# Attention's weight products: seven float32 quarter products replaced by three passes of 11-bit parts

## The chip, the cores and the metric

The kernel runs on one core of one Trainium2 chip. The metric is the time of one launch in microseconds (us), the median of several runs. All engines of the core work from their own instruction queues: TensorE (PE, with its weight loads shown apart as PEld), VectorE (DVE), ScalarE (ACT), GpSimd (POOL) and SyncE (SP, here a queue for DMAs).

## The reference

One transformer layer on 8192 tokens of 256 features, float32 in and out. `x` is `[4, 2048, 256]`; chunks are of 32 tokens.

```python
Q, K, V = x @ W_q.T, x @ W_k.T, x @ W_v.T
S = einsum('bncd,bnkd->bnck', Qc, Kc) * mask        # within chunks of 32, mask = decay ** distance
O = einsum('bnck,bnkd->bncd', S, Vc)
out = (sigmoid(x @ W_g.T) * O) @ W_o.T + x
x = layernorm(x + out)
h = silu(x @ wg.T) * (x @ wu.T)                     # 768 hidden, weights are integers / 127
x = layernorm(x + h @ wd.T)
```

## The kernel before

The tokens are taken in 16 blocks of 512. A block goes through attention two to three blocks ahead of its feed-forward part, so that one pass of the main loop (`b`) holds the feed-forward of block `b`, the scores, values and output product of block `n = b + 2`, and the weight products of block `m = b + 3`.

There are four attention weight products for each block, and they are what is changed. `y = M x` replaces Q and K (`M` is made once from both weights, `make_m`), `g` is the gate, `v` the values and `o` the output product. Feature-major products (`g`, `y`, helper `feature_major`, L455) leave features on partitions; token-major ones (`v`, `o`, helper `token_major`, L473) leave tokens on partitions. For block 0, and for the output product of blocks 0 and 15, they are plain float32 products of whole tiles (`attn_gate` L570, `attn_y` L589, `attn_v` L610, `attn_residual` through `project_back` L677, tile `pa`).

For the other blocks they go through `seven`: both factors are cut into 2 by 2 quarters, and seven float32 quarter products take the place of eight. `weight_sums` makes the sums of a weight's quarters once (POOL, five instructions of 128x128); `token_sums` makes four sums of 128x256 for each block of tokens (POOL), once for `x` and once for the gated values `goT`. `seven` opens four PSUM banks (`p1`, `p6`, `p5`, `p7`), runs four products, lets ACT copy two of the banks (L505) and DVE add them up (L507, L508) and POOL write one quarter of the result (L517); the closure `others` that it gives back runs the last three products onto the banks later and finishes the other quarters (L523, L526, L529, and L551 for the gate's sigmoids). Between the two halves of a set other PE work is put by hand.

The feed-forward part (`ffn_up` L790, `ffn_down` L677 and L856) already works with split operands: hidden states and activations are stored as a rounded high part (`F32R`, in the trace fp32r) and a rest in float16, and each product is run for both. In the trace a float32 product leaves two MATMUL rows and an fp32r or float16 product leaves one; MATMUL rows of fp32r operands are labelled f32 too, and are known by their tiles (`..._hi`).

The order within a queue is a scheduler's, but calls through `in_turn` keep the program's order on their engine, and `in_steady_turn` does so from block 1 on. The order of PE around the change is this, per pass of the loop:

```python
ffn_up(b, hT, uT, range(0, 1)); ffn_up(b, hT, uT, range(1, 2)); sT = attn_scores(n, yT)
ffn_up(b, hT, uT, range(2, 3)); v_next, v_rest = split_v(m, x_sums)
multiply = ffn_up(b, hT, uT, range(3, 4), held=True); v_rest(); multiply()
goT = attn_values(n, sT, v, sg); go_sums = token_sums(goT, f"go_{n}")
y_next, y_rest = split_y(m, x_sums); ffn_up(b, hT, uT, range(4, KH)); y_rest()
sg_next, g_rest = split_gate(m, x_sums); hs[n], out_rest = split_out(n, go_sums)
g_rest(); mv_h = out_rest()
x_sums = token_sums(xTs[m + 1], f"x_{m + 1}", in_turn); ffn_down(...)
```

Ahead of the loop, blocks 0 to 2 go through the same steps, with the weights' sums made first; PE is kept warm by six matmuls of zeros (`WARM`, L185) until the first data has landed.

Of the kernel before, what the change touches and what calls it, by code (L numbers as in the profile page):

```python
# [47 lines left out]
F32 = mybir.dt.float32  # L48
# [6 lines left out]
P = 128  # L55
# [3 lines left out]
TB = 512  # L59
# [7 lines left out]
HALF = 0.5  # L67
WARM = 512, 512, 128
# [3 lines left out]
def kernel(  # L72
# [353 lines left out]
    def weight_sums(w, name):  # L426

        a11, a21 = w[:, 0, :P], w[:, 0, P:]
        a12, a22 = w[:, 1, :P], w[:, 1, P:]
        t = const.tile([P, 5, P], F32, tag=f"{name}_sums", name=f"{name}_sums")  # L430
        s1, s2, s3, s4, minus = (t[:, i, :] for i in range(5))
        nc.gpsimd.tensor_tensor(s1, a21, a22, ALU.add)
        nc.gpsimd.tensor_tensor(s3, a11, a21, ALU.subtract)
        nc.gpsimd.tensor_tensor(s2, s1, a11, ALU.subtract)
        nc.gpsimd.tensor_tensor(s4, a12, s2, ALU.subtract)
        nc.gpsimd.tensor_scalar(minus, a22, -1.0, None, ALU.mult)
        return a11, a12, s4, minus, s1, s2, s3

    def token_sums(t, name, order=free):

        out = sums.tile([P, 4, HB], F32, tag=f"{name[0]}_sums", name=f"{name}_sums")
        t1, t3, t2, t4 = (out[:, i, :] for i in range(4))
        b11, b12, b21, b22 = (t[:, k, n * HB : (n + 1) * HB] for k in range(2) for n in range(2))
        order(nc.gpsimd.tensor_tensor(t1, b12, b11, ALU.subtract))
        nc.gpsimd.tensor_tensor(t3, b22, b12, ALU.subtract)
        nc.gpsimd.tensor_tensor(t2, b22, t1, ALU.subtract)
        nc.gpsimd.tensor_tensor(t4, t2, b21, ALU.subtract)
        return b11, b21, b22, t4, t1, t2, t3

    def feature_major(a, b):  # L450


        def product(i, pb, first, order=free):
            order(
                nc.tensor.matmul(  # L455
                    pb,
                    lhsT=a[i - 1],
                    rhs=b[i - 1],
                    start=first,
                    stop=True,  # L460
                    skip_group_check=True,
                )
            )

        return product

    def token_major(a, b):


        def product(i, pb, first, order=free):  # L470
            for g in range(HB // P):
                order(
                    nc.tensor.matmul(  # L473
                        pb[:, g * P : (g + 1) * P],
                        lhsT=b[i - 1][:, g * P : (g + 1) * P],
                        rhs=a[i - 1],
                        start=first and g == 0,
                        stop=True,
                        skip_group_check=True,
                    )  # L480
                )

        return product

    def seven(name, product, quarter, func=AF.Copy, plus=None):

        def shaped(t, like):
            return t.rearrange("p (g d) -> p g d", d=P) if len(like.shape) == 3 else t

        def part(what):
            return sums.tile([P, HB], F32, tag=what, bufs=2, name=f"{what}_{name}")

        banks = {i: bank(f"p{i}_{name}")[:, :HB] for i in (1, 6, 5, 7)}
        p = {}  # L500
        for i, pb in banks.items():
            product(i, pb, True)
            if i in (1, 5):
                p[i] = part(f"p{i}")
                nc.scalar.copy(p[i], pb)  # L505
        u, p57 = part("p6"), part("p57")
        in_steady_turn(nc.vector.tensor_tensor(u, banks[6], p[1], ALU.add))  # L507
        in_steady_turn(nc.vector.tensor_tensor(p57, banks[7], p[5], ALU.add))  # L508
        c11, c12, c21, c22 = (quarter(i, j) for i in range(2) for j in range(2))
        to_c12 = to_c21 = u  # L510
        if plus is not None:
            x11, x12, x21, x22 = (plus(i, j) for i in range(2) for j in range(2))
            to_c12, to_c21 = part("to_c12"), part("to_c21")
            for t, xq in ((to_c12, x12), (to_c21, x21)):
                nc.gpsimd.tensor_tensor(shaped(t, xq), shaped(u, xq), xq, ALU.add)
            nc.gpsimd.tensor_tensor(shaped(p57, x22), shaped(p57, x22), x22, ALU.add)
        nc.gpsimd.tensor_tensor(c22, shaped(p57, c22), shaped(u, c22), ALU.add)  # L517

        def others():
            for i, onto in ((2, 1), (3, 5), (4, 7)):  # L520
                product(i, banks[onto], False, in_turn)
            if plus is None:
                nc.scalar.activation(c11, shaped(banks[1], c11), func)  # L523
            else:
                in_steady_turn(
                    nc.vector.tensor_tensor(c11, shaped(banks[1], c11), x11, ALU.add)  # L526
                )
            for c, pb, t in ((c12, banks[5], to_c12), (c21, banks[7], to_c21)):
                in_steady_turn(nc.vector.tensor_tensor(c, shaped(pb, c), shaped(t, c), ALU.add))  # L529

        return others

    def by_features(t):
        return lambda i, j: t[:, i, j * HB : (j + 1) * HB]

    def by_tokens(t):
        per = NG // 2
        return lambda i, j: t[:, j * per : (j + 1) * per, i * P : (i + 1) * P]


    w_sums = {}

    def split_gate(b, x_sums):
        sg = work.tile([P, KD, TB], F32, tag="sg", name=f"sg_{b}")
        product = feature_major(w_sums["g"], x_sums)
        others = seven(f"g_{b}", product, by_features(sg), AF.Sigmoid)

        def rest():
            others()
            for raw in (sg[:, 0, HB:], sg[:, 1, :]):  # L550
                nc.scalar.activation(raw, raw, AF.Sigmoid)  # L551

        return sg, rest

    def split_y(b, x_sums):
        yT = work.tile([P, KD, TB], F32, tag="yT", name=f"yT_{b}")
        return yT, seven(f"y_{b}", feature_major(w_sums["m"], x_sums), by_features(yT))

    def split_v(b, x_sums):
        v = work.tile([P, NG, D], F32, tag="v", name=f"v_{b}")  # L560
        return v, seven(f"v_{b}", token_major(w_sums["v"], x_sums), by_tokens(v))

    def attn_gate(b):
# [4 lines left out]
        for ec in range(KD):  # L568
            for dc, pg in enumerate(banks):
                product = nc.tensor.matmul(  # L570
                    pg,
                    lhsT=wg[:, ec, dc * P : (dc + 1) * P],
                    rhs=xt[:, ec, :],
                    start=(ec == 0),
                    stop=(ec == KD - 1),
                )
                in_turn(product)
# [4 lines left out]
    def attn_y(b, beside=None):  # L582
# [3 lines left out]
        for fc in range(KD):  # L586
            py = bank(f"py_{b}_{fc}")
            for ec in range(KD):
                nc.tensor.matmul(  # L589
                    py,  # L590
                    lhsT=m_sb[:, ec, fc * P : (fc + 1) * P],
# [9 lines left out]
    def attn_v(b):  # L601
# [3 lines left out]
        for h in range(NG // per):  # L605
            pv = bank(f"pv_{b}_{h}")
            for j in range(per):
                g = h * per + j
                for ec in range(KD):
# [3 lines left out]
                        rhs=wv[:, ec, :],  # L613
# [31 lines left out]
    def attn_values(b, sT, v, sg):  # L645
        goT = work.tile([P, KD, TB], F32, tag="goT", name=f"goT_{b}")
# [45 lines left out]
    def attn_residual(b, goT):  # L692
# [7 lines left out]
        project_back(b, (chunked(goT),), (chunked(wo),), residual, "pa")  # L700
# [7 lines left out]
    def split_out(b, goT_sums):  # L708
# [3 lines left out]
        product = token_major(w_sums["o"], goT_sums)  # L712
        others = seven(f"o_{b}", product, by_tokens(r), plus=by_tokens(xn))

        def rest():
            others()
            return moments(r, f"a{b}")
# [183 lines left out]
    table = const.tile([P, 1], F32, tag="table", name="table")  # L901
    hs, hTs = {}, {}
    sg, v = attn_gate(0), attn_v(0)
    for w, name in ((wg, "g"), (wv, "v")):
        w_sums[name] = weight_sums(w, name)
    x_sums = token_sums(xTs[1], "x_1")
    make_m()
    w_sums["m"] = weight_sums(m_sb, "m")
    in_turn(nc.scalar.mul(wo, wo, HALF))
    w_sums["o"] = weight_sums(wo, "o")  # L910
    sg_1, g_rest = split_gate(1, x_sums)
    fg = integers(ffn_gT, ffn_int[0], "fg")
    look_up([0])
    yT = attn_y(0, lambda half: look_up([1 + half]))
    g_rest()
    look_up([3])
    v_1, rest = split_v(1, x_sums)
# [4 lines left out]
    yT, rest = split_y(1, x_sums)  # L922
# [3 lines left out]
    hs[0] = attn_out(0, goT)  # L926
    sT_1 = attn_scores(1, yT)
    xTs[3] = load_xT(3)
    x_sums = token_sums(xTs[2], "x_2")
    v, rest = split_v(2, x_sums)  # L930
    goT = attn_values(1, sT_1, v_1, sg_1)
    go_sums = token_sums(goT, "go_1")
    rest()
    yT, rest = split_y(2, x_sums)
# [3 lines left out]
    hs[1], out_rest = split_out(1, go_sums)  # L938
    sg, g_rest = split_gate(2, x_sums)
# [12 lines left out]
    for b in range(NB - 2):  # L952
# [12 lines left out]
        if b == 0:  # L965
            g_rest()
            x_sums = token_sums(xTs[m], f"x_{m}")
# [12 lines left out]
        if more:  # L980
            v_next, v_rest = split_v(m, x_sums)
# [10 lines left out]
        if b == 1:  # L992
            count = count_wide()
            n_wide_early = const.tile([1, 1], I32, tag="n_wide_early", name="n_wide_early")
            nc.vector.tensor_copy(n_wide_early, count)
        if more:
            go_sums = token_sums(goT, f"go_{n}")
            y_next, y_rest = split_y(m, x_sums)
# [318 lines left out]
```

## Time and profile before

| what | value |
|---|---|
| time of a launch, median of 3 runs | 524.65 us (523.93 to 524.71) |
| span of the profiled execution, first to last instruction | 522.4 us |
| what lies around the span (median less span) | 2.25 us |
| PE busy | 515.8 us, 99% |
| DVE, POOL, ACT busy | 389.8, 343.5, 320.4 us |
| mean granted TensorE clock | 0.998 |
| one pass of the loop, in the middle of the run | 31.6 us |
| busy in the pass from 233.60 to 265.20 | PE 31.60, DVE 23.49, ACT 19.85, POOL 21.80 us |

The page gives the profiled execution no other time than its span. "Chain" is the chain of work that ended last, followed back from the last instruction. Rows of a group give how many instructions there were and the mean time of one in ns; PE's rows overlap, because its matmuls are pipelined, so PE's cost is read from start to start or from the chain.

### The profile page before, as it was taken

To read this page: it belongs to the slowest core of one execution; us is meant where nothing else is said; L and a number is where in the kernel's file an instruction comes from. 1 tells how busy PE (TensorE), PEld (TensorE's weight loads), DVE (VectorE), ACT (ScalarE), POOL (GpSimd) and SP (SyncE) were. 2 spreads that over 40 slices of the span, in tenths; PEclk is the share of its full clock that TensorE was granted. 3 is DMA by queue.
4 is the path that set the end of the run, shared out by engine and by line. 5 is a ranking of instruction groups with operands and counts; after the bars stand their busy time and mean duration, and the time that the engine had idled before them with its cause. 6 is when DMAs were issued, how large, how long until landed. Compare 5 with 4: busy or idle time off the path is not lost.

```text
span 522.4 us, 10573 instructions
## 1 busy us (share of the span) xinstructions
PE 515.8 (99%) x3648; PEld 421.8 (81%) x3648; DVE 389.8 (75%) x965; ACT 320.4 (61%) x644; POOL 343.5 (66%) x475
## 2 busy tenths in 40 slices
PE   9999999999999999999999999999999999999995
PEld 5798887887978788887888878889787888878685
DVE  3978797686776867868677776877868677787876
ACT  2755565465656756666675665656566566667746
POOL 6535785776847668485675856678486685836554
PEclk9999999999999999999999999999999999999999
DMA  7721121213213131131311313141121311102102
GB/s 246 234 83 43 51 62 29 63 42 76 89 32 90 52 112 41 39 95 45 106 43 45 119 25 97 44 117 43 35 89 51 110 43 40 44 21 62 62 23 81
DMA packets 43320, 36.90 MB, mean 71 GB/s; under 512 B 4864, under 2 KB 39168, under 8 KB 43264
## 3 DMA queue, kind: packets, MB, share of 16 engines
q1 hardware_dynamic: 42144, 35.28, 22.6%
q10 hardware_dynamic: 1120, 0.92, 0.5%
q8 instruction: 30, 0.49, 0.4%
q14 instruction: 26, 0.21, 0.1%
HBM read 20.45 MB, written 8.39 MB: 55 GB/s over the span
## 4 chain that ended last, share of the span: by engine, by line
PE 98%; DVE 1%; ACT 0%; issue 0%
PE fg L790 17%; PE fu L790 16%; PE fdn L677 14%; PE p_v L473 9%; PE p_y L455 9%; PE p_g L455 9%; PE p_o L473 8%; PE po L651 5%; PE ps L630 3%; PE fdn L856 2%; PE pa L677 1%; PE pi L185 1%; PE pv L610 1%; PE pg L570 1%; PE py L589 1%; PE fdn L1125 1%
## 5 line engine op out<-in xcount | busy, mean ns | idle before, releaser
L815 POOL TENSOR_TENSOR u_lo<-u,u_hi 128x512 f16<-128x512 f32 (+1 forms) x98 | 122.9, 1256 | 111.2 <-ACT u_hi L814 109.7
L814 ACT CAST u_hi<-u 128x512 fp32r<-128x512 f32 (+1 forms) x98 | 59.7, 609 | 67.0 <-DVE u L812 66.6
L800 DVE SCALAR_TENSOR_TENSOR s<-fg,s 128x512 f32<-128x512 f32 (+1 forms) x98 | 66.2, 677 | 33.5 <-ACT s L798 33.4
L798 ACT ACTIVATE s<-fg 128x512 f32<-128x512 f32 (+1 forms) x98 | 55.9, 582 | 40.7 <-PE fg L790 40.7
L812 DVE TENSOR_TENSOR u<-fu,s 128x512 f32<-128x512 f32 (+1 forms) x98 | 66.5, 679 | 10.4 <-POOL u_lo L815 1.1
L790 PE MATMUL fg<-hT_hi,fg_hi 128*128 128x512 f32 (+1 forms) x196 | 73.8, 458 | 0.0
L790 PE MATMUL fu<-hT_hi,fu_hi 128*128 128x512 f32 (+1 forms) x196 | 60.5, 390 | 0.0
L790 PE MATMUL fg<-hT_lo,fg_lo 128*128 128x512 f16 (+1 forms) x196 | 57.9, 377 | 0.0
L790 PE MATMUL fu<-hT_lo,fu_lo 128*128 128x512 f16 (+1 forms) x196 | 57.4, 375 | 0.0
L677 PE MATMUL fdn<-fd_hi,u_hi 128*128 128x256 f32 x312 | 45.7, 288 | 0.0
L790 PEld LDWEIGHTS fu<-hT_hi,fu_hi 128*128 128x128 f32 x196 | 36.5, 188 | 8.4
L410 ACT ACTIVATE h<-h,shift_h,scale_h 128x256 f32<-128x256 f32 x52 | 27.0, 590 | 24.1 <-POOL shift_h L373 24.1
L790 PEld LDWEIGHTS fg<-hT_hi,fg_hi 128*128 128x128 f32 x196 | 34.6, 189 | 8.9
L677 PEld LDWEIGHTS fdn<-fd_hi,u_hi 128*128 128x128 f32 x312 | 38.9, 189 | 0.3
L677 PE MATMUL fdn<-fd_lo,u_lo 128*128 128x256 f16 x312 | 38.6, 273 | 0.0
L790 PEld LDWEIGHTS <-fu_lo 128*128 128x128 f16 x196 | 19.2, 98 | 22.2
L773 POOL TENSOR_TENSOR hT_lo<-hT,hT_hi 128x512 f16<-128x512 f32 x28 | 35.3, 1280 | 1.2 <-ACT hT_hi L772 1.2
L838 DVE SCALAR_TENSOR_TENSOR r<-fdn,h 128x512 f32<-128x512 f32 x30 | 20.7, 689 | 20.4 <-PE fdn L677 18.0
L790 PEld LDWEIGHTS <-fg_lo 128*128 128x128 f16 x196 | 15.3, 98 | 20.7 <-issue 12.9
L473 PE MATMUL p_v<-v_sums,x_sums 128*128 128x128 f32 x240 | 31.8, 275 | 0.0
L677 PEld LDWEIGHTS <-u_lo 128*128 128x128 f16 x312 | 28.4, 98 | 3.9
L651 PE MATMUL po<-sT,v 128*128 128x128 f32 x256 | 31.2, 275 | 0.0
(210 smaller groups left out, 1182.7 us busy)
## 6 DMA issues: line engine op xcount, KB each, us to landing
x<-in_x_dram SPq DMA_DIRECT2D x16, 512.0 KB, 3.4
xT<-in_xT_dram SPq DMA_DIRECT2D x15, 512.0 KB, 4.2
hT<-sq SPq DMA_DIRECT2D x224, 32.0 KB, 1.9
out_dram<-r SPq DMA_DIRECT2D x13, 512.0 KB, 4.5
out_dram<-r SPq DMA_DIRECT2D x7, 128.0 KB, 1.7
fg_int<-in_ffn_gT_dram SPq DMA_DIRECT2D x3, 256.0 KB, 8.5
fu_int<-in_ffn_uT_dram SPq DMA_DIRECT2D x3, 256.0 KB, 7.2
fd_int<-in_ffn_dT_dram SPq DMA_DIRECT2D x3, 256.0 KB, 5.9
```

The source lines that it names most:

```text
L410: nc.scalar.activation(r[:, g, :], r[:, g, :], AF.Identity, bias=shift[:, g : g + 1], scale=scale[:, g : g + 1],)
L455: nc.tensor.matmul(pb, lhsT=a[i - 1], rhs=b[i - 1], start=first, stop=True, skip_group_check=True,)
L473: nc.tensor.matmul(pb[:, g * P : (g + 1) * P], lhsT=b[i - 1][:, g * P : (g + 1) * P], rhs=a[i - 1], start=first and g == 0, stop=True, ski ...
L651: nc.tensor.matmul(po[:, cols], lhsT=v[:, g, dc * P : (dc + 1) * P], rhs=sT[:, cols], start=True, stop=True,)
L677: nc.tensor.matmul(pb[:, j * D : (j + 1) * D], lhsT=part[:, g * P : (g + 1) * P], rhs=w, start=(i == 0), stop=(i == len(terms) - 1),)
L773: nc.gpsimd.tensor_tensor(in_order[1], whole, in_order[0].bitcast(F32), ALU.subtract)
L790: nc.tensor.matmul(pb, lhsT=w[kind][:, dc, hc * P : (hc + 1) * P], rhs=hT[kind][:, dc, cols], start=(kind == kinds[0] and dc == 0), stop=( ...
L798: order(nc.scalar.activation(s, pg, AF.Sigmoid, scale=SCALE / H_UP))
L800: gated = nc.vector.scalar_tensor_tensor(s, pg, U_UP / H_UP**2, s, ALU.mult, ALU.mult)
L812: in_steady_turn(nc.vector.tensor_tensor(u, pu, s, ALU.mult))
L814: nc.scalar.copy(hi, u)
L815: nc.gpsimd.tensor_tensor(lo, u, hi.bitcast(F32), ALU.subtract)
```

## The change

Each operand is split into a high part, rounded to fp32r, and a scaled low part. The product is `hi*hi + lo*lo` and a third product of differences that supplies both mixed terms (Karatsuba): three passes, each over the whole operand, all in fp32r. After the first two passes the PSUM bank is scaled in place by ACT (`WHOLE`), and the third pass is added onto it. The sets are used where `seven` was, and also for the output product of block 15, where `attn_residual` was.

```diff
+SHIFT = 2.0**12
+TOP = 1.0 - 0.5 / SHIFT
+WHOLE = 1.0 + 1.0 / SHIFT
...
+    def weight_parts(w, name, tags):
+        hi, lo = (const.tile([P, KD, D], F32R, ...) ...)
+        nc.scalar.mul(hi, w, TOP)
+        nc.gpsimd.tensor_tensor(lo, w, hi.bitcast(F32), ALU.subtract)
+        nc.gpsimd.tensor_scalar(lo, lo.bitcast(F32), SHIFT, None, ALU.mult)
+        return [hi, lo]
+
+    def weight_gap(parts, name):
+        nc.gpsimd.tensor_tensor(gap, hi.bitcast(F32), lo.bitcast(F32), ALU.subtract)
+        parts.append(gap)
+
+    def token_parts(t, name, order=free):
+        for k in range(KD):
+            order(nc.scalar.mul(hi[:, k, :], t[:, k, :], TOP))
+            whole = hi[:, k, :].bitcast(F32)
+            order(nc.gpsimd.tensor_tensor(lo[:, k, :], t[:, k, :], whole, ALU.subtract))
+            in_steady_turn(
+                nc.vector.scalar_tensor_tensor(
+                    gap[:, k, :], whole, -WHOLE, t[:, k, :], ALU.mult, ALU.add
+                )
+            )
...
     def feature_major(a, b):
+        def product(i, pb, kind, order=free):
+            for k in range(KD):
+                order(nc.tensor.matmul(pb, lhsT=a[kind][:, k, i * P : (i + 1) * P],
+                                       rhs=b[kind][:, k, :], start=kind + k == 0, ...))
     def token_major(a, b):
+        per = TB // D
+        def product(i, pb, kind, order=free):
+            for k in range(KD):
+                for j in range(per):
+                    g = i * per + j
+                    order(nc.tensor.matmul(pb[:, j * D : (j + 1) * D],
+                                           lhsT=b[kind][:, k, g * P : (g + 1) * P],
+                                           rhs=a[kind][:, k, :], start=kind + k + j == 0, ...))
-    def seven(name, product, quarter, func=AF.Copy, plus=None):
...
+    def three(name, product, finish):
+        banks = [bank(f"p{i}_{name}") for i in range(2)]
+        for i, pb in enumerate(banks):
+            product(i, pb, 0)
+            product(i, pb, 1)
+            in_steady_turn(nc.scalar.mul(pb, pb, WHOLE))
         def others():
+            for i, pb in enumerate(banks):
+                product(i, pb, 2, in_turn)
+                finish(i, pb)
         return others
...
-    for w, name in ((wg, "g"), (wv, "v")):
-        w_sums[name] = weight_sums(w, name)
-    x_sums = token_sums(xTs[1], "x_1")
+    for name in ("wg", "wv"):
+        w_parts[name] = weight_parts(given[name], name, (f"{name}_hi", f"{name}_lo"))
+        weight_gap(w_parts[name], name)
+    x_parts = token_parts(xTs[1], "x_1")
...
-            hs[n] = attn_residual(n, goT)
-            mv_h = moments(hs[n], f"a{n}", order=in_turn)
+            hs[n], out_rest = split_out(n, go_parts)
+            mv_h = out_rest(in_turn)
```

`finish` is a sigmoid by ACT for `g` (two of 128x512), a copy by DVE for `y`, a copy by ACT for `v`, and an addition of `x` by DVE for `o`. The tile `goT` has one buffer where it had two. A branch that runs only for integer weights above 128 gets its float32 weights back from the parts; with these inputs it does not run.

## The prediction

> **What bounds the kernel now.** I read the busy shares first, then the chain by engine, then the chain in order of time for one pass of the loop, then PE's timeline for the pace of fp32r, and last the groups by form for the other engines. Busy shares and chain of the page:
>
> ```profile
> PE 515.8 (99%) x3648; PEld 421.8 (81%) x3648; DVE 389.8 (75%) x965; ACT 320.4 (61%) x644; POOL 343.5 (66%) x475
> PE 98%; DVE 1%; ACT 0%; issue 0%
> ```
>
> PE never waits; a change pays as far as it shortens PE's work, and costs as far as it makes PE wait. The chain in order of time (start, us) shows what PE spends in a pass on the weight products:
>
> ```profile
> 13.79 1.73 PE p_g L455 x8
> ...
> 245.82 1.78 PE p_v L473 x16
> 249.40 1.34 PE p_v L473 x12
> 250.74 1.79 PE po L651 x16
> 252.52 1.73 PE p_y L455 x8
> 257.86 1.29 PE p_y L455 x6
> ...
> 265.30 5.43 PE fdn L677 x48
> ...
> 487.21 0.47 PE fu L790 x2
> 487.68 0.45 PE fg L790 x2
> 488.12 0.43 PE fu L790 x2
> ```
>
> A feature-major set costs 1.73 + 1.29 = 3.02 us, a token-major one 1.78 + 1.34 = 3.12. The last three lines give the pace of 512 columns: two fp32r matmuls in 0.47, two float16 ones in 0.43 to 0.45. For 256 columns PE's timeline has, start to start (1.50 us for twelve fp32r):
>
> ```profile
> 235.47 1.65 PE L677 MATMUL fdn<-fd_hi,u_hi 128*128 128x256 f32 x12
> 236.97 1.48 PE L677 MATMUL fdn<-fd_lo,u_lo 128*128 128x256 f16 x12
> ```
>
> **PE's work.** A set becomes three passes over whole operands. Feature-major: 3 x 2 banks x 2 = 12 matmuls of 512 columns, 12 x 0.235 = 2.82 us, 0.20 less. Token-major: 24 of 256 columns. Their price lies between 0.113 (5.43 / 48, half of it float16) and 0.125 (1.50 / 12); I take 0.12, since `u_hi` is loaded as these weights will be: 2.88 us, 0.24 less. Blocks 1 to 15 have `y`, `g`, `v`: 30 x 0.20 + 15 x 0.24; `o` runs for 14 blocks: 14 x 0.24; block 15's `pa` goes from 3.46 to 2.88. Sum 6.0 + 3.6 + 3.4 + 0.6 = **13.6 us less**; at 0.125 and 0.113 it is 10.0 and 18.6.
>
> **The other engines, per pass.** POOL loses eight token sums, four corner sums and three additions of x, 15 x 0.73 = 11.0, and gains four low parts of 1.28: 21.8 becomes 15.9. DVE loses 17 additions of 0.42 and gains four gaps, two copies of `y` and two additions of `x` at about 0.68: 23.5 becomes 21.8. ACT loses eight copies (0.37), three finishes (0.38) and two sigmoids (0.42, 0.63), 5.1 us, and gains eight scalings, two sigmoids and two copies at 0.585 and four high parts at 0.61, 9.5 us: 19.9 becomes 24.2 of 30.7. No engine becomes the bound by its sum. The 0.585 is this row, which reads PSUM and writes SBUF; no row has ACT writing PSUM:
>
> ```profile
> L617 ACT COPY v<-pv 128x512 f32<-128x512 f32 x2 | 1.2, 585 | 1.3 <-PE pv L610 1.3
> ```
>
> The bounds are 0.55 (the pace of neighbouring ACT rows) and 0.69 (DVE on the same bank). [...]
>
> **The new waits, start.** Before, block 1's gate set starts at 13.79, on sums that POOL had made by 14.1 as they were needed. Now, by the order in the program, POOL makes the low parts of two weights, scales both, makes both gaps, and only then `x_1_lo`. Each is 128x512: a subtraction 1.28; a scaling has no row: 128x128 takes 0.525 and 128x4 0.22, so 1.47 by that slope, bounds 1.28 (a subtraction) and 2.1 (four times 0.525). ACT's first table load stands behind the landing of `wg` (about 5.4): load 1.28, `wg_hi` 0.62, done at 7.3; `wv_hi` stands behind a second load and the decay (9.2): 9.8. POOL: `wg_lo` at 8.6, `wv_lo` 11.1, two scalings 14.0, two gaps 16.6, `x_1_lo` 17.9 and 19.1. PE finishes the two `hi` matmuls at 14.26, waits 3.6 us, runs one, waits 1.0: **4.6 us** (bounds 3.9 and 5.9). Behind it on PE all is queued in order. Later, `x_2_hi` stands behind ACT's casts of the integer weights and `x_2_lo` (two of 1.28) behind it: 0.5 us. The scalings of the other early sets end before PE asks.
>
> The idle PE brings in its clock. At the end of the run the last matmul ended at 516.8, and the windows read 1.00 until 520, 0.97 to 520.5 and then:
>
> ```profile
> 520.50:521.00 0.50, 0.00 (x0) 0.00 (x0) 0.00 (x0) 0.00 (x0) 0.00 (x0) 0.50 0.81 268
> ```
>
> So 3.7 us of idleness halved it. Here the unbroken wait is 3.6: I take no drop, but it is at the edge; the six warm-up matmuls took 4.18 us where full pace gives 2 x 0.86 + 0.22 = 1.94, so a drop costs up to 2.2. [...]
>
> **The new waits, a pass.** The third pass of a bank waits for ACT's scaling. For `y` it comes 3.6 us after the second pass, hidden by two chunks; for `g` and `o` I find 0.5 us of slack or more. The tight one is `v`: only chunk 3 and one `po` matmul lie between. From the end of `fdn`, PE reaches it after 1.80 + 1.80 + 1.08 + 1.95 + 1.92 + 1.80 + 0.22 = 10.57 us. ACT's queue has the scaling behind `u_hi` of chunk 2, which ends a DVE chain: by DVE's timeline, start to start: residual and two gaps 3 x 0.61 + 0.04 = 1.87 (the gaps are new there), statistics 1.00, transposes 1.38, two chunks 2.80, mask 0.70, chunk 2 1.52, so `u` is done at 9.27; then ACT: cast 0.55 and scaling 0.58, 10.4, the second 10.95 against 11.05. The waits nearly vanish; I put 0.15 on each of 12 passes, 1.8 us, for what a semaphore takes; bounds 0 and 0.6. In block 15's output nothing lies between the passes, and the scalings stand behind `u_hi` of chunk 5: the last is done 3.5 after the set's start, the last two matmul groups end at 4.0, not 2.88: 1.1 us. One buffer for `goT` costs nothing: its readers are done a pass earlier. No DMA is added, removed or moved past another on SP's queue.
>
> **Sum.** -13.6 + 4.6 + 0.5 + 1.8 + 1.1 = -5.6 on a span of 522.4, 516.8; with 2.25 around it **519.0 us**. About 0.2% (1 us) is what a measurement of this kernel can tell from no change.
>
> **Rivals.** (a) *Slower: ACT becomes late at the v set.* ACT gains 4.3 us in each pass, and the scaling stands behind a DVE chain with two gaps in it. From 0.62 us of wait per pass (1.8 + 5.6 = 7.4 over 12) nothing is left; at 0.9 it is -5.6 - 1.8 + 10.8, 528. For it: the slack is 0.1. Against it: DVE's other work falls by 1.7 and POOL's by 5.9. (b) *The passes save nothing*: fp32r weights at every matmul hold the pace to 0.25 and 0.13 (the first pairs after a change of type take 0.66 for two); the sets cost 3.0 and 3.1 and of the 13.6 some 0.9 is left against 8.0 of waits: about 532. Against it: twelve in a row hold 0.125. (c) *More*: 0.113 and no waits in a pass give -18.6 + 6.2, 512. For it: in the last chunks, two fp32r matmuls of 256 columns start 0.23 apart. (d) That the clock drops in the wait adds 2 us to any of these.
>
> **How the numbers follow.** Forecast 0.50, (a) 0.24, (b) 0.08, (c) 0.18. The forecast's own range, by the bounds, is 514 to 523.5; the range reaches into (a) and (c): 513 to 528. Faster: 0.44 of the forecast and (c), 0.62; same: 0.03 of it and 0.05 of (a), 0.08; slower: 0.30.
>
> **What would show it.** Right: a pass of 30.7 to 31.0 us in the chain; p_y and p_g 1.88 + 0.94, p_v and p_o 1.92 + 0.96; one wait of PE on POOL `x_1_lo` of over 3 us near 14 us; ACT 24 us in a pass. Wrong: PE waits on ACT's scaling in every pass, a set over 3.0 us on PE, or a granted clock under 1 in the loop.

## The result, and the profile after

The changed kernel takes 547.54 us (median of 4 runs, 547.5 to 547.98) against 524.61 us of the kernel before in the same series: the ratio is 1.0441, 95% interval 1.0429 to 1.0454. It is 22.9 us slower; 519.0 was forecast, and the range ended at 528. The profiled execution has a span of 546.4 us, 24.0 more than before, and a mean granted clock of 0.985.

Busy shares, and the shares of the chain by engine, on the page of the changed kernel:

```profile
PE 509.4 (93%) x3480; PEld 404.2 (74%) x3480; DVE 398.7 (73%) x833; ACT 375.9 (69%) x696; POOL 295.3 (54%) x310
PE 62%; DVE 26%; ACT 3%; issue 3%; DMA 2%; POOL 1%; SPq 1%; DVEq 1%; ACTq 0%
```

PE's work did fall, by 6.4 us in this count. But PE no longer carries the chain: DVE holds 26% of it, where it held 1%. The waits of PE (us in total, times, longest) say where PE stands:

```profile
PE p_v L494 <- ACT p_v L513: 17.6, 12, 1.5
PE p_g L472 <- POOL x_lo L458: 5.1, 2, 4.6
PE p_o L494 <- POOL go_lo L458: 1.9, 2, 1.2
PE p_o L494 <- ACT p_o L513: 1.4, 1, 1.4
```

The first is a wait of 1.5 us in each of 12 passes: the third pass of the `v` set waits for ACT's scaling. ACT is only the last link. The chain in order of time, one pass:

```profile
180.37 5.44 PE fdn L663 x48
186.45 2.67 DVE x_gap L460 x2
190.12 1.42 DVE sq L739 x4
195.16 0.70 DVE s L791
195.99 0.70 DVE u L803
197.87 1.22 PE p_v L494 x8
...
200.65 1.86 PE p_y L472 x8
206.13 0.93 PE p_y L472 x4
...
212.67 5.44 PE fdn L663 x48
```

From the down projection it runs through DVE: two gaps in 2.67 us, transposes, the chunks' activations, then ACT's cast and scaling, then PE. The sets themselves cost what was forecast here: 1.86 + 0.93 for `p_y`. The timelines of DVE, ACT and PE show where the chain starts and ends (start and duration in us):

```profile
185.84 0.69 DVE L829 SCALAR_TENSOR_TENSOR r<-fdn,h 128x512 f32<-128x512 f32 x1 [0.96 <-PE fdn L663]
189.04 0.74 DVE L327 BATCH_NORM_STATS2 st_f<-r 128x6 f32<-128x256 f32 x2
...
196.71 0.62 ACT L805 CAST u_hi<-u 128x512 fp32r<-128x512 f32 x1 [1.69 <-DVE u L803]
197.24 1.06 ACT L513 ACTIVATE p_v<-p_v 128x512 f32<-128x512 f32 x2
197.87 1.22 PE L494 MATMUL p_v<-wv_gap,x_gap 128*128 128x256 f32 x8 [1.47 <-ACT p_v L513]
```

The groups of the two instructions that split a tile (busy us and mean ns behind the bar) show the odd price:

```profile
L458 POOL TENSOR_TENSOR go_lo<-goT,go_hi 128x512 fp32r<-128x512 f32 x30 | 50.3, 1696 | 19.6 <-ACT go_hi L456 19.6
L458 POOL TENSOR_TENSOR x_lo<-xT,x_hi 128x512 fp32r<-128x512 f32 x30 | 43.8, 1481 | 17.9 <-ACT x_hi L456 17.5
L460 DVE SCALAR_TENSOR_TENSOR x_gap<-x_hi,xT 128x512 fp32r<-128x512 f32 x30 | 36.8, 1259 | 0.0
L460 DVE SCALAR_TENSOR_TENSOR go_gap<-go_hi,goT 128x512 fp32r<-128x512 f32 x30 | 34.9, 1203 | 23.0 <-ACT go_hi L456 23.0
```

A gap takes 1.20 to 1.26 us where 0.61 to 0.68 was put, and POOL's subtraction beside it 1.48 to 1.70 where 1.28 was.

Split at the first instruction of the down projections (from PE's timeline), with what the prediction's terms make of each stretch:

| stretch | before | after | difference | predicted |
|---|---|---|---|---|
| start to block 0's down projection | 75.08 | 82.90 | +7.8 | +2.7 |
| 12 passes, to block 12's | 379.54 | 387.95 | +8.4 | -8.8 |
| to block 13's | 22.65 | 27.12 | +4.5 | +0.5 |
| from there to the end | 45.13 | 48.43 | +3.3 | 0 |

The start has its own reason beside the wait for `x_1_lo`. Busy us of PE, PEld, DVE, ACT and POOL in stretches, then the granted clock and the DMA share:

```profile
14.00:18.00 4.00, 0.00 (x0) 0.00 (x0) 3.99 (x12) 1.25 (x3) 3.92 (x4) 1.00 1.10 348
18.00:22.00 4.00, 3.00 (x6) 2.11 (x7) 3.99 (x7) 1.11 (x2) 3.91 (x4) 0.51 0.33 108
22.00:25.00 3.00, 3.00 (x5) 1.30 (x4) 2.83 (x5) 2.67 (x6) 2.83 (x3) 0.52 0.00 0
```

PE stands still from 14 to 18 us, and then the clock is halved for 7 us. `py`, 3.43 us before, takes 4.78. In the same way the windows from 496 to 499 us read 0.50, after the waits of block 15's output product, of which none is longer than 1.4 us.

Of the 3.3 us at the end, 0.4 to 0.6 are such half-clock time (a down projection of 6.08 us in place of 5.51). Most of the rest comes after the last output is sent off. PE's sequencer jumps over the branch that does not run, first in the trace before, then after (min, median, max in ns):

```profile
L1255 PEldq COMPARE_BRANCH  x2: 95/252/410, 519.7 to 520.0; - x2
L1251 PEldq COMPARE_BRANCH  x2: 91/2203/4315, 540.9 to 541.2; - x2
```

The jump takes 4.3 us instead of 0.4; the other engines' jumps take 0.04 to 0.06 us in both. The last output is sent off 5.9 us before the end of the span, where it was 3.0.

### The profile page after: what moved, and what is told of

Same layout as the page of the kernel before. It is cut to its first block, busy times and chain, and to the rows that moved or that the text cites. A ratio compares the mean times of both kernels' runs of the same rounds, so it can differ in the third digit from the quotient of the medians.

```text
span 546.4 us, 9719 instructions
## 1 busy us (share of the span) xinstructions
PE 509.4 (93%) x3480; PEld 404.2 (74%) x3480; DVE 398.7 (73%) x833; ACT 375.9 (69%) x696; POOL 295.3 (54%) x310
## 3 DMA queue, kind: packets, MB, share of 16 engines
q1 hardware_dynamic: 42144, 35.28, 21.8%
## 4 chain that ended last, share of the span: by engine, by line
PE 62%; DVE 26%; ACT 3%; issue 3%; DMA 2%; POOL 1%; SPq 1%; DVEq 1%; ACTq 0%
PE fdn L663 13%; PE p_g L472 8%; PE p_o L494 8%; PE p_y L472 7%; PE fg L781 7%; PE fu L781 7%; DVE x_gap L460 6%; DVE u L803 5%; DVE s L791 5%; PE po L637 4%; PE p_v L494 4%; DVE sq L739 3%; PE fdn L847 2%; DVE sT L627 2%; ACT u_hi L805 2%
## 5 line engine op out<-in xcount | busy, mean ns | idle before, releaser
L781 PE MATMUL fg<-hT_hi,fg_hi 128*128 128x512 f32 (+1 forms) x196 | 71.3, 445 | 0.0
L458 POOL TENSOR_TENSOR go_lo<-goT,go_hi 128x512 fp32r<-128x512 f32 x30 | 50.3, 1696 | 19.6 <-ACT go_hi L456 19.6
L458 POOL TENSOR_TENSOR x_lo<-xT,x_hi 128x512 fp32r<-128x512 f32 x30 | 43.8, 1481 | 17.9 <-ACT x_hi L456 17.5
L460 DVE SCALAR_TENSOR_TENSOR go_gap<-go_hi,goT 128x512 fp32r<-128x512 f32 x30 | 34.9, 1203 | 23.0 <-ACT go_hi L456 23.0
L702 DVE TENSOR_TENSOR h<-p_o,x 128x512 f32<-128x512 f32 x30 | 19.4, 686 | 36.0 <-PE p_o L494 31.8
L663 PE MATMUL fdn<-fd_hi,u_hi 128*128 128x256 f32 x312 | 44.6, 285 | 0.0
L460 DVE SCALAR_TENSOR_TENSOR x_gap<-x_hi,xT 128x512 fp32r<-128x512 f32 x30 | 36.8, 1259 | 0.0
L494 PE MATMUL p_v<-wv_gap,x_gap 128*128 128x256 f32 x120 | 18.1, 294 | 17.6 <-ACT p_v L513 17.6
```

What stands on the lines that cost most here:

```text
L458: order(nc.gpsimd.tensor_tensor(lo[:, k, :], t[:, k, :], whole, ALU.subtract))
L460: nc.vector.scalar_tensor_tensor(gap[:, k, :], whole, -WHOLE, t[:, k, :], ALU.mult, ALU.add)
L494: nc.tensor.matmul(pb[:, j * D : (j + 1) * D], lhsT=b[kind][:, k, g * P : (g + 1) * P], rhs=a[kind][:, k, :], start=kind + k + j == 0, sto ...
L663: nc.tensor.matmul(pb[:, j * D : (j + 1) * D], lhsT=part[:, g * P : (g + 1) * P], rhs=w, start=(i == 0), stop=(i == len(terms) - 1),)
L781: nc.tensor.matmul(pb, lhsT=w[kind][:, dc, hc * P : (hc + 1) * P], rhs=hT[kind][:, dc, cols], start=(kind == kinds[0] and dc == 0), stop=( ...
```

## The experiments

The theory to be tested: **two engines exclude each other.** A DVE instruction with two inputs in SBUF and a POOL instruction do not run at once; each waits for the other's whole instruction. By it the gap (1.20 to 1.26 us) pays for POOL's subtraction (1.48 to 1.70), DVE's chain gets longer, and the `v` set is late. The rivals: the gap is slow by itself; or ACT's scaling is the late one whatever DVE does. Apart from that, three smaller losses were to be told apart: the start, block 15 and the jump. The next table has the stretches of all runs, from the profiled execution of each; the launch is the median of several, and the ratio is to the kernel before, with its 95% interval.

| run | launch us | ratio | to block 0 | 12 passes | block 13 | rest |
|---|---|---|---|---|---|---|
| after | 547.54 | 1.0441 (1.0429-1.0454) | 82.90 | 387.95 | 27.12 | 48.43 |
| e1_scale_first | 529.53 | 1.0086 (1.0057-1.0115) | 83.00 | 369.67 | 27.87 | 48.76 |
| e2_hi_for_lo | 526.48 | 1.0018 (0.9994-1.0042) | 80.65 | 371.44 | 26.00 | 48.11 |
| e3_plain_15 | 541.36 | 1.0329 (1.0312-1.0347) | 81.58 | 387.87 | 22.57 | 47.78 |
| e4_start | 549.83 | 1.0480 (1.0463-1.0498) | 84.49 | 387.91 | 27.12 | 48.98 |
| e5_start_act | 542.37 | 1.0351 (1.0328-1.0374) | 79.27 | 387.85 | 26.30 | 47.68 |
| e6_all | 520.05 | 0.9922 (0.9904-0.9940) | 78.46 | 369.72 | 22.57 | 47.85 |
| e7_all_pad | 520.27 | 0.9927 (0.9911-0.9944) | 81.10 | 369.68 | 22.64 | 45.08 |
| e8_gap_pool | 530.27 | 1.0123 (1.0100-1.0145) | 82.53 | 370.45 | 28.01 | 47.41 |
| e9_all_tail | 517.99 | 0.9890 (0.9874-0.9906) | 78.52 | 369.87 | 22.60 | 45.31 |

**Is the price of the gap POOL's company?** (e2_hi_for_lo)

```diff
-            order(nc.gpsimd.tensor_tensor(lo[:, k, :], t[:, k, :], whole, ALU.subtract))
...
-        return hi, lo, gap
+        return hi, hi, gap
```

> Edit: POOL makes no low part of the tokens and of goT; the second pass takes the high part in its place (so the low parts' product is left out of the result), with as many matmuls of the same shape. DVE's gap is the same instruction as before, only without POOL's subtraction beside it. Theory A (DVE's instruction with two inputs in SBUF and POOL's instructions exclude each other, so the gap pays POOL's time too): mean of a gap 0.61-0.70 us instead of 1.20-1.26, a pair 1.25-1.35 instead of 2.4-2.7; PE's wait for p_v falls from 1.5 us a pass to 0-0.3; with the wait for x_1_lo at the start gone too (some 8 us), the launch takes 518-528. Rival B (1.2 us is the instruction's own time): the gaps stay at 1.2 us, PE's wait for p_v at 1.5 us, and only the start's 8 us are gained: 538-541.

The gaps' groups without POOL beside them:

```profile
L459 DVE SCALAR_TENSOR_TENSOR go_gap<-go_hi,goT 128x512 fp32r<-128x512 f32 x30 | 20.6, 726 | 23.0 <-ACT go_hi L456 23.0
L459 DVE SCALAR_TENSOR_TENSOR x_gap<-x_hi,xT 128x512 fp32r<-128x512 f32 x30 | 19.9, 695 | 0.7 <-ACT x_hi L456 0.7
```

The same instruction takes 0.70 to 0.73 us. PE's wait for `p_v` falls from 17.6 to 0.3 us in all and a pass from 32.3 to 30.9. The gap is not slow by itself; that rival falls. A pair of gaps in the loop takes 1.28 us here and 2.67 there, and 1.4 us is about the wait that each pass had. At the start only 2.3 of the 8 us came back that were expected: with the low part gone PE waits for `yT` instead (3.4 and 1.0 us), and the stretch to block 0 takes 80.65 us; the mean granted clock of this execution is 0.985 (0.998 before the change).

**Does it matter only because of ACT's order?** (e1_scale_first)

```diff
-        ffn_up(b, hT, uT, range(2, 3))
+        multiply = ffn_up(b, hT, uT, range(2, 3), held=True)
...
             v_next, v_rest = split_v(m, x_parts)
+        multiply()
         multiply = ffn_up(b, hT, uT, range(3, 4), held=True)
```

> Edit: chunk 2's second multiplication (u, with its cast u_hi by ACT) is taken after the first half of the v set, so that ACT's two scalings of p_v stand ahead of u_hi of chunk 2. Nothing is left out. Theory A (PE's 1.5 us of wait in each of 12 passes is the scaling standing behind a cast that waits for DVE's late chain): the wait goes, a pass falls from 32.3 to 30.7-31.0 us, the launch from 547.5 to 529-532. The gaps' rows stay at 1.20-1.26 us. Rival (another wait takes its place, for chunk 2's or 3's activations ahead of the down projection): less than half of the 17.6 us comes back, the launch stays above 539.

The gaps stay at 1.20 to 1.24 us, the wait is gone, a pass takes 30.80 us and the launch 18.0 less. So in a pass the long gap costs only where a PE product stands behind it: the scaling itself was ready to run, but queued behind a cast that waited for DVE. With the order changed the chain of the whole run is 91% PE again. Nothing took the place of the wait.

**Can the gap leave DVE instead?** (e8_gap_pool)

```diff
-            in_steady_turn(
-                nc.vector.scalar_tensor_tensor(
-                    gap[:, k, :], whole, -WHOLE, t[:, k, :], ALU.mult, ALU.add
-                )
-            )
+            order(nc.scalar.mul(gap[:, k, :], whole, -1 / SHIFT))
+            order(
+                nc.gpsimd.tensor_tensor(
+                    gap[:, k, :],
+                    gap[:, k, :].bitcast(F32),
+                    lo[:, k, :].bitcast(F32),
+                    ALU.add,
+                )
+            )
```

> Edit: the tokens' gap is made without DVE: ACT writes the high part times -1/4096, POOL adds the low part. Nothing is left out; the order of the v set is that of the changed kernel. ACT has four instructions of 0.57 us more in a pass, two of them ahead of block b+1's first sigmoid, POOL four of 1.28 us. Theory A (DVE's gap in POOL's company is what makes the v set late): DVE's chain is 2.6 us shorter and ACT's 1.15 longer, PE's wait for p_v falls from 1.5 us to 0-0.3 a pass, a pass takes 30.8-31.1, the launch 528-534. Rival (ACT is the late one, as the slower rival of the prediction had it): the wait for p_v grows to 2 us or more, a pass takes over 32.5, the launch over 549.

Four more instructions on ACT and on POOL, none on DVE: the passes take 370.5 us and the wait for `p_v` is 0.6 us in all. ACT, with 2.5 us more work in a pass, was not late; the rival that has ACT as the cause falls. With no gap on DVE beside them, POOL's instructions take 1.28 to 1.29 us:

```profile
L461 POOL TENSOR_TENSOR x_gap<-x_gap,x_lo 128x512 fp32r<-128x512 f32 x30 | 38.4, 1282 | 2.2 <-POOL minus_mean_h L404 0.6
```

**Block 15** (e3_plain_15): its output product is the float32 product again.

```diff
-        go_parts = token_parts(goT, f"go_{n}")
         if more:
+            go_parts = token_parts(goT, f"go_{n}")
...
-            hs[n], out_rest = split_out(n, go_parts)
-            mv_h = out_rest(in_turn)
+            hs[n] = attn_residual(n, goT)
+            mv_h = moments(hs[n], f"a{n}", order=in_turn)
```

> Edit: block 15's output product is the plain float32 product again (tile pa), with no parts of its goT; its weight is put together from the two parts by POOL in the pass before, 2.8 us beside other work. Theory A (the last stage waits for the go parts at 488-496 us and PE's clock drops after it): the stretch from the down projection of block 12 to that of block 13 falls from 27.2 to about 22.8-23.5, the last down projections from 6.08 to 5.5 us, and the launch by 5-8 us, to 540-543. Rival (the waits there come from the feed-forward chain of that block): a loss of 0.6 on PE's work and a gain of under 2: 546-548.

The stretch to block 13's down projection takes 22.57 us, a little under what was expected and less than before the change (22.65), though the set has 3.46 us of PE where three passes have 2.9. The launch is inside its range; 1.3 us of its gain stand at the start, which the edit leaves alone: there the wait and the half clock came out shorter (3.3 and 3.4 us in place of 4.6 and 6.8). The chain there:

```profile
488.92 3.46 PE pa L663 x16
492.37 5.51 PE fdn L847 x48
```

The 0.6 us that three passes save here had cost 4.5: nothing lies between the parts of `goT` and the products that use them.

**The start** (e4_start): `x_1_lo` ahead of the value weight's parts and of both gaps.

```diff
+    w_parts["wg"] = weight_parts(wg, "wg", ("wg_hi", "wg_lo"))
     x_parts = token_parts(xTs[1], "x_1")
+    w_parts["wv"] = weight_parts(wv, "wv", ("wv_hi", "wv_lo"))
     make_m()
...
     sg_1, g_rest = split_gate(1, x_parts)
+    weight_gap(w_parts["wg"], "wg")
+    weight_gap(w_parts["wv"], "wv")
```

> Edit: POOL makes block 1's low part straight after the gate weight's first subtraction; the value weight's parts and both weights' gaps come behind it. Nothing is left out. Theory A (PE's 4.6 + 0.4 us of wait for x_1_lo at 14 us is POOL's queue alone, and the clock falls because of that wait): the wait is under 1.2 us, the eight py matmuls after it take 3.4-3.6 instead of 4.8-5.0 us, the granted clock from 18 to 27 us is 1.00 instead of 0.51-0.71, and the launch is 6-8.5 us shorter, 539-541.5. Rival (the clock falls for another reason, such as the loads of the first 18 us): py stays near 4.8 us and 4-5 us are gained: 542.5-543.5. Neither touches the passes: PE's wait for p_v stays at 1.5 us.

A miss for both. The wait for `x_1_lo` is 0.7 us, and `py` runs at full clock (3.6 us), but the launch takes 2.3 us more than the changed kernel. PE's waits have a new line, the scores on `yT`:

```profile
PE ps L616 <- DVE yT L582: 4.5, 2, 3.7
```

DVE copies `yT` at the end of a queue of small mask instructions. DVE and POOL there, in the timeline (start and duration in us):

```profile
14.80 1.33 DVE L244 SCALAR_TENSOR_TENSOR factor<-bit,decay,factor 128x32 f32<-128x32 f32 x1
14.81 1.28 POOL L458 TENSOR_TENSOR x_lo<-xT,x_hi 128x512 fp32r<-128x512 f32 x1
...
16.05 1.29 POOL L438 TENSOR_TENSOR wv_lo<-wv,wv_hi 128x512 fp32r<-128x512 f32 x1
16.06 1.32 DVE L244 SCALAR_TENSOR_TENSOR factor<-bit,power,factor 128x32 f32<-128x32 f32 x1
...
17.30 1.27 POOL L446 TENSOR_TENSOR wg_gap<-wg_hi,wg_lo 128x512 fp32r<-128x512 f32 x1
17.31 1.31 DVE L245 TENSOR_TENSOR chunk_mask<-chunk_mask,factor 128x32 f32<-128x32 f32 x1
...
18.54 0.17 DVE L241 CAST bit<-bit_int 128x32 f32<-128x32 int32 x1
```

This is the clearest sight of the mechanism. A DVE instruction on 32 columns, which takes 0.2 us otherwise, is recorded with 1.3 us and ends 0.04 to 0.05 us after the POOL instruction that began with it; then both start their next one together. The DVE instruction waits out a whole POOL instruction, at 32 columns too. But a wait for a whole instruction shows only beside POOL's instructions with two inputs. Beside a scaling, which has one (1.50 us here), the gap keeps its time, 0.68 us:

```profile
13.23 1.50 POOL L439 TENSOR_SCALAR wg_lo<-wg_lo 128x512 fp32r<-128x512 f32 x1
13.88 0.68 DVE L460 SCALAR_TENSOR_TENSOR x_gap<-x_hi,xT 128x512 fp32r<-128x512 f32 x1
```

In all traces together, 21 gaps had only one-input POOL instructions beside them and took 0.66 to 0.80 us; small DVE instructions took 0.17 to 0.68 there. PE idles from 24 to 27.5 us, and the clock is 0.50 from 27.5 to 34: the loss of the changed kernel's start, 10 us later.

**The start once more** (e5_start_act): as e4, and ACT copies block 0's `yT`.

```diff
-            nc.vector.tensor_copy(yT[:, fc, :], py)
+            nc.scalar.copy(yT[:, fc, :], py)
```

> Edit: that of e4_start, and block 0's two copies of yT are made by ACT instead of DVE, so that the scores don't wait behind DVE's mask chain (small DVE instructions that each wait for a POOL instruction of 1.3 us). Nothing is left out. Theory A (in e4 the 4.5 us of wait only moved from x_1_lo to yT, and the clock fell after it as before): now neither wait is there, no stretch of the start has a granted clock under 0.9, and the down projection of block 0 starts at 75.5-78 us instead of 82.9 (e4: 84.5); the launch is 540-543. Rival (the wait moves on once more, to the mask itself, which the scores' product with the values needs): a wait of over 3 us on sT at 26-32 us, block 0 starts at 81 us or later, the launch is over 545.

No wait of PE at the start is over 1.7 us, and the granted clock stays at 1.00 until the run's end. The launch is inside the expectation (542.37); block 0's down projection, at 79.27, is 1.3 us later than expected, since waits of 1.7 on `sT` (DVE's mask chain again) and 1.3 and 0.9 on low parts by POOL remain.

**All three together** (e6_all).

> Edit: e1_scale_first, e3_plain_15 and e5_start_act together. Nothing is left out. Theory A (three separate losses, which add up): block 0's down projection at 76-78 us, 12 passes in 369.7 us (30.8 each), block 13's stretch 22.6, the rest 47.8: span 516-518, launch 517-520, that is 0.987-0.992 of the kernel before. Rival (they share a resource, and a mended wait brings another out): 524 or more.

The losses add up: 520.05 us, 0.05 over the expected range, since block 0's down projection comes 0.5 us late; the other stretches are as expected, and the granted clock has no drop before PE's work is done:

```profile
PEclk9999999999999999999999999999999999999998
```

**The jump** (e7_all_pad): e6 with more instructions in PE's queue, 34 small matmuls (pads) in place of the three of `WARM` and 34 behind the last down projection. The question is whether PE's jump, 0.41 us before the change and 4.3 after it, changes with their number alone.

```diff
-    for n in WARM:
+    def pad(count, n, order, pi=pi):
+        for _ in range(count):
...
+    pad(34, 128, lambda ins: None)
...
         down_products(g, terms)
+    pi = bank("pi_last")
+    pad(34, 8, in_turn, pi)
```

> [...] The time of the launch is not what is asked here, since the pads take up to 3 us of PE at each place: 515-523.

```profile
L1266 PEldq COMPARE_BRANCH  x2: 95/255/415, 515.9 to 516.2; - x2
```

The jump takes 0.42 us and the end of the run 2.8 less (45.08 against 47.85). In e1 to e6 and e8 it took 3.8 to 4.3. So its price changed with the number of PE instructions ahead of it, while what is in the branch stayed the same. No run shows what PE does in the 3.4 to 3.9 us between. The launch gains nothing, because the start lost 2.6 us. That is not the missing warming, since PE reaches block 1's gate set within 0.1 us of e6: DVE has four reductions between the mask and `sT` where e6 has two, PE waits 2.2 us for it where it waited 1.1, and the clock is halved for 3.4 us behind this wait (windows as above):

```profile
27.00:30.00 3.00, 0.87 (x4) 0.38 (x2) 2.97 (x6) 3.00 (x7) 1.57 (x2) 1.00 0.31 119
31.00:33.50 2.50, 2.50 (x13) 2.50 (x12) 0.69 (x1) 2.50 (x6) 0.31 (x1) 0.50 0.00 0
```

**The pads where PE is idle** (e9_all_tail): warming as it was, 62 pads behind the last down projection.

> Edit: e6_all with the three warming matmuls left as they are and 62 tiny bfloat16 matmuls behind the last down projection, where PE has nothing left to do (34 of them took 1.0 us in e7). Theory: PE's jump over the branch takes about 0.4 us as in e7, the start is that of e6 (block 0's down projection at 78-79 us), the end is 2.5-2.8 us shorter: span 515.5-516.5, launch 516.8-518.0, ratio to the kernel before 0.985-0.988. [...]

The jump takes 0.80 us, the rest 45.31. The launch takes 517.99 us, just inside the expectation: 0.9890 of the kernel before (0.9874 to 0.9906; 0.985 to 0.988 was expected), some 5.3% less than the changed kernel by the two ratios. It is the fastest of all that were run. The three passes are a gain of 1.1%, once little waits for their parts; some 4 us of waits are left at the start.

## Why the prediction was wrong, step by step

Between the two spans, 29.6 us separate forecast and measurement: 17.2 in the 12 passes, 5.1 at the start, 4.0 at block 15 and 3.3 at the end.

**PE's work: right in the passes.** A pass with no wait takes 30.80 us (e1, e6), 0.79 less than 31.59; 0.88 was put. In e6's chain the sets cost 1.88 + 0.93 for `y` and 1.87 + 1.11 for `g` (put: 1.88 + 0.94), and 1.88 + 0.94 for `v` and 1.88 + 0.98 for `o` (put: 1.92 + 0.96). Rival (b), that the passes save nothing, falls; so does (c). At the start the sets saved less: PE is busy for 73.26 us up to block 0's down projection in e6, where the clock is whole, and for 74.08 before: 0.8 in place of 2.4. Why the early sets cost more was not tested.

**The v set: the failed step.** Its term "residual and two gaps 3 x 0.61 + 0.04 = 1.87" was mis-sized. From the end of the down projection at 185.64 the parts were, put and measured: residual and gaps 1.87 and 3.20; statistics 1.00 and 1.08; transposes 1.38 and 1.35; two chunks 2.80 and 2.81; mask 0.70 and 0.88; chunk 2 1.52 and 1.55; and 0.20 before the first that was not put. So `u` is done at 11.07 and not at 9.27, 1.33 of the 1.80 by the gaps alone. PE reached the set at 10.76 (put: 10.57). It waited 1.47 us; 0.15 was put, an allowance that comes from no row, with a bound at 0.6. That is 17.6 us in the place of 1.8. It is rival (a), named with its place and its break-even of 0.62 us, but priced at 0.9 and given 0.24. Its name for the cause, a late ACT, was right only in that ACT is the last link: e8 gave ACT more work and the wait went.

The 0.61 came from a DVE row with one input in PSUM. The gap has both inputs in SBUF, and the steady pass before had no such row. The trace before did have the warning, in its mask chain; DVE's timeline and POOL's:

```profile
11.89 0.75 DVE L236 CAST bit<-bit_int 128x32 f32<-128x32 int32 x1
```

```profile
11.88 0.72 POOL L445 TENSOR_TENSOR x_sums<-xT 128x256 f32<-128x256 f32 x1
```

The same cast takes 0.17 us at 13.37 us. "Bounds from the nearest rows" should have taken this pair: a gap beside a 1.28 us subtraction can cost up to 0.61 + 1.28, an estimate from these rows and POOL's subtraction. With 1.26 for each gap the prediction's own chain gives 10.57, 11.7 with ACT's two instructions, a wait of 1.1 us and a slower kernel. With both inputs in SBUF and a POOL instruction with two inputs beside it, the wait is up to one whole instruction of POOL (a gap of 0.68 us took 1.76 at most, the mask's 0.2 us became 1.3). DVE instructions with one input in PSUM (`s`, `u`) kept their 0.65 to 0.69 us while POOL ran.

**The start: the wait right in sum, the clock wrong.** 3.6 and 1.0 us were put for the two low parts and 0.5 for `x_2_lo`; 4.6, 0.4 and 0.2 came. (Waits of 0.8 us for `sT` and 0.5 for `h` were not put.) The sum is right (5.1 and 5.3), but the unbroken piece is 1.0 longer, since POOL ended `x_1_lo` at 18.5 and not at 17.9, and PE was ready at 13.95 and not at 14.26. So "no drop, but at the edge" fell on the other side: half a clock from 18 to 25 us. This is rival (d), put at +2 for any case.

The prediction asked whether one unbroken wait was long enough, and that was the wrong question. Waits of 3.3 us (e3), 3.7 (e4) and 4.6 (after) were each followed by 3.4 or 6.8 us at 0.50, but so were the 2.2 us of e7 and, at block 15, the 2.8 of e2; in the changed kernel the clock fell there among three waits of 0.8, 1.2 and 1.4 us, and the same three in e5 left it whole. What sorts them is this. In every trace the clock changes at whole multiples of 3.41 us from the first clock record. Cut at these multiples up to PE's last matmul, the traces have 11 stretches at full clock in which PE was idle for 1.95 us or more in sum, and each is followed by one at half clock; with 1.66 us or less none is. Where the multiples fall differs between executions: e2's launches took 522.0 to 527.7 us, at mean clocks of 0.995 to 0.985. A stretch at half clock is followed by another where PE was idle in it for 0.54 us or more (6 times), and by full clock at 0.18 or less (11 times). In the changed kernel the idle time in these stretches was 3.41 and 1.97 us ahead of the two drops and 1.52 at most where the clock stayed whole; in e4 two waits of 0.79 and 1.16 made up the 1.95. By this count a wait of 3.6 us leaves at least 1.8 in one stretch, and the next of 1.0 adds to it: a drop was the likely case. The changed kernel lost two stretches at the start, 6.83 us at 0.50, since PE was idle for 0.95 us in the first.

**Block 15: the place right, the size wrong.** 1.1 us was put for ACT's last scaling. But the low parts of `goT` by POOL were late first (1.9 us of wait; 1.70 each, beside the gaps), ACT's scaling cost 1.4 more, and the clock fell behind them: the stretch is 4.5 us longer.

**The end: not put at all.** It costs some 2.7 us by PE's jump (e6, whose last products run at full clock: 47.85 against 45.13). A change to the count of PE's instructions was not seen as a term.

**The other engines.** A pass has 23.1 us of ACT (put: 24.2), 23.7 of DVE (21.8) and 17.9 of POOL (15.9); four gaps at 1.23 in place of 0.68 are DVE's 2 us too many. ACT's rows were priced right: a scaling, PSUM to PSUM, takes 0.562 to 0.572 us (put: 0.585), a copy of the same bank to SBUF 0.588.

## What to carry to other kernels

Price a DVE instruction by a row with the same homes of its inputs, and with POOL busy beside it as it will be: with two inputs in SBUF beside a POOL instruction with two inputs, the gap took 1.20 to 1.26 us in the mean and 1.76 at most, and 0.70 to 0.73 without (e2). A sum of engine times does not show this; follow the chain that ends at the tightest product, and put the instruction that releases PE ahead of those that wait for a longer chain. Where PE must wait, add up its idle time over stretches of 3.41 us, at whose ends the clock changed here: waits of 0.79 and 1.16 us in one stretch were followed by half clock (e4) as one of 4.6 was (the changed kernel), and where the waits fall in these stretches differs from run to run.

## What the runs showed of the hardware

- DVE's instructions with both operands in SBUF and POOL's with two inputs took turns by whole instructions, and small instructions suffered most: 0.17 to 0.24 us became 1.22 to 1.35 when POOL worked on 128x512. Beside POOL's scalings (one input) a gap took its 0.66 to 0.80 us. Which property decides was not tested by itself. In the changed kernel the mask's casts (0.18 to 0.45 us otherwise, 1.25 to 1.31 beside a POOL instruction with two inputs), copies (0.22 to 0.66, and 1.34) and multiplications (0.18 to 0.30, and 1.22) in SBUF waited; instructions on 128x512 that read PSUM (0.65 to 0.69), transposes (0.40 to 0.45) and reductions (0.68) took the same time either way.
- PE's jump over code that does not run took 0.4 to 0.8 us (before, e7, e9) or 3.8 to 4.3 (the other runs); 124 more instructions ahead of it (62 matmuls and their weight loads), in an idle place, took 2.5 us off the end (e9 against e6).
- The clock changed at multiples of 3.41 us, and the idle time of PE in such a stretch sorts the changes: 1.95 us in sum was followed by a stretch at 0.50, 1.66 was not; what lies between no run shows.
- Half-clock time can outlast the wait that set it off: 2.2 us of wait and 3.4 us at 0.50 (e7), 4.6 and 6.8 (the changed kernel).
